# A graph network with sorted neighbour lists: heavy and light sorts as two stages, and a dense stage that starts ahead of its load

## The chip, the cores and the metric

The kernel runs on one core of a Trainium2 chip. A core has a matrix engine (PE; its weight loads are shown apart as PEld), a vector engine (DVE), an activation engine (ACT), a general engine (POOL) and a queue engine (SP) that here only issues DMAs. Each takes its instructions in the order in which the program has them and waits where one isn't ready. The metric is the device time of one call, in microseconds (us); lower is better.

## The reference, cut to what matters

A batch of 16 graphs, 1024 nodes, 64 channels, goes through four layers; each adds its result to x. All layers use the same adjacency matrix of a graph (1024 x 1024 float32, 4 MB a graph).

```python
h = relu(layernorm(x)); x = x + L0(h, adj)   # m = two dense layers of h; msg = relu(adj @ m); GRU cell of msg and h
h = relu(layernorm(x)); x = x + L1(h, adj)   # relu(D^-1/2 (adj + I) D^-1/2 (h @ kernel))
h = relu(layernorm(x)); x = x + L2(h, adj, nodemask)
h = relu(layernorm(x)); x = x + L3(h, adj)   # ((adj + I) @ h) / row sums
# L2: per node, a list of neighbours (its own node among them, some struck out by a dilation rule);
# per channel, the neighbours' values are sorted, and three quantiles are added up:
sv = sort(where(valid, x[:, None], big), axis=2)
agg = 0.25 * q(0.25) + 0.5 * q(0.5) + 0.25 * q(0.75)      # linear interpolation between two sorted values
out = (x + agg) @ W1 -> relu -> @ W2
```

The sort of L2 is what the change is about: every node has its own list, and all 64 channels of it are sorted apart.

## The kernel before, in words

Nodes are ranked by degree. The 128 nodes of highest degree ("heavy", in six classes, table HEAVY) have long lists; the seven other groups of 128 ("light") have at most 13 entries. A graph goes through stages, each written as a generator:

- fetch and load: the adjacency comes in as eight tiles of 128 x 1024 (tile a), PE transposes them, ACT copies them out (strip) and makes signs of them (sgn), and SP stores the transpose to DRAM (adjT).
- code, rank, cut, list: from the signs come degrees, ranks, the dilation and at last the lists of indices, idxH for heavy and idxL for light nodes, and weights that stand for the three quantiles.
- mid (`middle`, `dense01`, lines 1288 to 1382): layers 0 and 1. X is loaded, layernorm gives hm, two products give m2x; then adjT is read back in eight tiles (am) for the first adjacency product; the GRU cell (tiles rz, nn, d0) updates X; a second layernorm (tr), the second adjacency product, and X again; X is stored (x1), and a third layernorm's result h2 (another hm) is stored as the table tab.
- gath (`gathers`): POOL fetches rows of tab by index with indirect DMAs, one for 128 rows: 34 for the heavy lists into gh, which PE transposes and ACT copies into hb0; then 32 for the first light net into s0, 22 for the second into s1.
- sort (`sorts`): a heavy sort (tiles hb0 and hb1 in turn), then two light sorts (s0 with o0, s1 with o1). The steps are minima and maxima on DVE. hb1, o0 and o1 share one buffer, by the tag "other".
- sums: light keys are weighted (ACT) and added (DVE), and stored as agg; the heavy ones are summed within their sort.
- rear (`dense23`): layers 2 and 3; POOL gathers agg into rank order (zz, 8 indirect DMAs), then dense products, a layernorm (hr) and the third adjacency product, and the output.

No loop runs these. All stages of all 16 graphs go into one list at build time. `Order.run` (lines 223 to 248) takes again and again the stage whose next step can start first by the build's own estimate, and lets it issue that step; on a tie the earlier one in the list wins, which is sorted by the table `first` (0 for rear, sums and gath, 1 for mid and the lists, 2 for loads, 7 for the sorts). `yield after("name")` holds a stage back until the named stage or mark is done. So the order of instructions on each engine is fixed when the program is built, and any edit to stages, marks or buffers can move all of it. On the chip nothing is reordered.

Buffers: a tile's `bufs` says how many of it are there; the next one in turn waits for the readers of the one whose place it takes. LIGHTBUFS gives s0 and s1 two each, hb0 has two, X two, the t2 tiles of mid (nn, d0, tr, u1) two in common.

Every engine call goes through one helper, so the profile gives line 388 for nearly all instructions; they are told apart by their tiles.

Of the kernel before, what the change touches and what calls it, by code (L numbers as in the profile page):

```python
# [18 lines left out]
P = 128  # L19
EPS = 1e-5  # L20
STRIP = 1
DEPTH = 5
LIGHTBUFS = (2, 2)
SGN = 2
AM = 3
GH = 4
# [367 lines left out]
def kernel(  # L394
# [117 lines left out]
    def lists_for_all():  # L512
# [12 lines left out]
        def bank(dtype=F32):  # L525
            return ps1.take([P, 512 * 4 // mybir.dt.size(dtype)], dtype, "bank")
# [658 lines left out]

        def layernorm_relu(X, h=None, who="m", times=None):

            yield "V", X
            s = wp.tile([P, NT], F32, name="ln_s", bufs=2)
            V.reduce_sum(s, X, AX.X)  # L1190
            V.tensor_scalar(s, s, -1.0 / H, None, ALU.mult)
            yield "A", s
            v = wp.tile([P, NT], F32, name="ln_v", bufs=2)
            if h is None:
                h = wp.tile([P, NT, H], F32, name="h" + who, bufs=1)
            for t in range(NT):
                A.activation(h[:, t, :], X[:, t, :], AF.Square, bias=s[:, t : t + 1], accum_out=v[:, t : t + 1])
            A.activation(v, v, AF.Sqrt, bias=eps, scale=1.0 / H)
            yield "V", v
            V.reciprocal(v, v)  # L1200
            if times is not None:
                V.tensor_mul(v, v, times)
            V.tensor_mul(s, s, v)
            yield "A", s, v
            for t in range(NT):
                A.activation(h[:, t, :], X[:, t, :], AF.Relu, bias=s[:, t : t + 1], scale=v[:, t : t + 1])
            return h
# [4 lines left out]
                A.activation(dst[:, t, :], src[:, t, :], func, scale=by[:, t : t + 1])  # L1212

        def t2(name, who="m"):
            return wp.tile([P, NT, H], F32, name=name, tag="t2" + who, bufs=2 if who == "m" else 1)

        def transposed(h, dst):
            for i in range(NH):
# [67 lines left out]
            return pm  # L1286

        def dense01(b, S):
            X = wp.tile([P, NT, H], F32, name="X", bufs=2)
            S_.dma_start(X, x[b].rearrange("(t p) h -> p t h", p=P))  # L1290

            h = yield from layernorm_relu(X)
            cat = wp.tile([P, N], F32, name="cat")
            yield from transposed(h, cat[0:H, :])
            yield "T", cat
            m1T = wp.tile([P, N], F32, name="m1T", tag="big")
            pm = yield from product(w1, cat[0:H])
            yield from evicted(pm, m1T[0:H], AF.Relu, b1)
            yield "T", m1T
            p2 = yield from bank()  # L1300
            T.matmul(p2, *bias(0), start=True, stop=False)
            ams = streamed(b, 0)
            for t in range(NT):
                o = p2[:, t * H : (t + 1) * H]
                T.matmul(o, m1T[0:H, t * P : (t + 1) * P], w2, start=False, stop=t == NT - 1)
            yield "A", p2
            A.activation(m2x[:, :, 0:H], p2.rearrange("p (t h) -> p t h", h=H), AF.Relu)
            ps1.close(p2)
            pm = yield from propagated(b, m2x, 0, ams)

            yield "A", pm
            A.copy(m1T[H : H + 1, :], pm[H : H + 1, :])
            yield from evicted(pm, cat[H:P], AF.Relu)
            yield "T", m1T
            pr = yield from bank()
            for t in range(NT):
                T.transpose(
                    pr[:, t : t + 1], m1T[H : H + 1, t * P : (t + 1) * P], ident[H : H + 1, H : H + 1]
                )
            yield "V", pr  # L1320
            S["rs"] = rs = st.tile([P, NT], F32, name="rs")
            V.tensor_scalar(rs, pr[:, 0:NT], 1.0, None, ALU.add)
            ps1.close(pr)
            rz = wp.tile([P, NT, 2 * H], F32, name="rz", tag="big")
            nn = t2("nn")
            for g in range(2):
                yield "T", cat
                pg = yield from bank2()
                for i in range(4):
                    t = 4 * g + i  # L1330
                    o = pg[:, i * 4 * H : (i + 1) * 4 * H]
                    if i % 2 == 0:
                        T.matmul(pg[:, i * 4 * H : (i + 2) * 4 * H], *bias(2), start=True, stop=False)
                    T.matmul(o, cat[:, t * P : (t + 1) * P], wg, start=False, stop=i % 2 == 1)
                pgv = pg.rearrange("p (i c) -> p i c", c=4 * H)
                gs = slice(4 * g, 4 * g + 4)
                yield "A", pg
                A.activation(rz[:, gs, :], pgv[:, :, 0 : 2 * H], AF.Sigmoid)
                yield "V", rz
                V.tensor_mul(nn[:, gs, :], pgv[:, :, 2 * H : G], rz[:, gs, 0:H])  # L1340
                V.tensor_add(nn[:, gs, :], nn[:, gs, :], pgv[:, :, G : 4 * H])
                ps2.close(pg)
            yield "A", nn
            A.activation(nn, nn, AF.Tanh)
            yield "V", nn

            d0 = t2("d0")
            V.tensor_sub(d0, h, nn)
            V.tensor_mul(d0, d0, rz[:, :, H : 2 * H])
            V.tensor_add(d0, d0, nn)  # L1350
            V.tensor_add(X, X, d0)

            ams = streamed(b, 1)

            dinv = wp.tile([P, NT], F32, name="dinv", bufs=2)
            V.tensor_scalar(dinv, rs, 1e-30, None, ALU.max)
            yield "A", dinv
            A.activation(dinv, dinv, AF.Sqrt)
            yield "V", dinv
            V.reciprocal(dinv, dinv)  # L1360
            V.scalar_tensor_tensor(dinv, rs, 0.0, dinv, ALU.is_gt, ALU.mult)
            tr = yield from layernorm_relu(X, t2("tr"), "m", dinv)
            pm = yield from propagated(b, tr, 1, ams, own=True)
            g0 = wp.tile([P, N], F32, name="g0", tag="big")
            yield from evicted(pm, g0[0:H])
            yield "T", g0
            pm = yield from product(wk, g0[0:H])
            g1 = wp.tile([P, N], F32, name="g1", tag="big")
            yield from evicted(pm, g1[0:H])
            pa = yield from back(g1[0:H])  # L1370
            yield "A", pa
            u1 = t2("u1")
            scaled(u1, pa, dinv, AF.Relu)
            ps1.close(pa)
            yield "V", u1
            V.tensor_add(X, X, u1)

            yield "S", X
            S_.dma_start(D[b % DEPTH]["x1"].rearrange("(t p) h -> p t h", p=P), X)
            h2 = yield from layernorm_relu(X)  # L1380
            yield "S", h2
            S_.dma_start(D[b % DEPTH]["tab"][1 : N + 1, :].rearrange("(t p) h -> p t h", p=P), h2)
# [7 lines left out]
        def gather_heavy(b, S):  # L1390
# [1 line left out]
            d = D[b % DEPTH]  # L1392
            idxH = S["idxH"]
            yield "P", D[b % DEPTH]["tab"], idxH
            S["hb"] = hb = [qp.tile([P, NSLOT], F32, name="hb0", bufs=2), None]
            base = 0
            for _, nr, k, s, _, _ in HEAVY:
                if s > k:
# [210 lines left out]
        def sort_light(b, S, g):  # L1609
            ts, kept, _ = NETS[g]  # L1610
            n, width = USED[ts[0]], len(ts) * H
            plan = nets[g][0]
            bufs = [S["s", g], qp.tile([P, n * width], F32, name=f"o{g}", tag="other")]
            far(bufs[1], g, 1)

            def view(bf, first, stp, nr, ln, c):
# [147 lines left out]
        def middle(b, S):  # L1764
            if b:
                yield after(f"mid{b - 1}")
            yield after(f"load{b}")
            yield from dense01(b, S)

        def gathers(b, S):  # L1770
            yield after(f"list{b}", f"mid{b}")
            if b:
                yield after(f"gath{b - 1}")
            if b >= 2:
                yield after(f"heavy{b - 2}")
            yield from gather_heavy(b, S)
            yield f"gh{b}"
            for g in range(len(NETS)):
# [4 lines left out]

        def sorts(b, S):
            if b:
                yield after(f"sort{b - 1}")
            yield after(f"gh{b}")
            yield from sort_heavy(b, S)
            yield f"heavy{b}"
            for g in range(len(NETS)):  # L1790
                yield after(f"gl{b}.{g}")
                yield from sort_light(b, S, g)
                yield f"light{b}.{g}"
# [13 lines left out]
        for b in range(B):  # L1807
            S = {}
            for name, stage in (
                ("rear", rear), ("mid", middle), ("fetch", fetching), ("load", loads), ("code", coding), ("rank", ranking), ("cut", cutting), ("list", listing),  # L1810
                ("gath", gathers), ("sort", sorts), ("sums", sums),
            ):
                order.add(f"{name}{b}", stage(b, S))
        first = {"rear": 0, "sums": 0, "gath": 0, "conv": 1, "mid": 1, "list": 1, "cut": 1, "rank": 1, "code": 1, "load": 2, "fetch": 2, "sort": 7}
        order.stages.sort(key=lambda q: first[q[0].rstrip("0123456789")])
        with tc.manual_schedule():
            order.run()
# [383 lines left out]
```

## Time and profile before

| what | value |
| --- | --- |
| median of three runs | 2703.5 us (2701.03 to 2710.99) |
| profiled execution: time, span from first to last instruction | 2704.4 us, 2702.6 us |
| mean granted PE clock in it | 0.767 |
| heavy minima and maxima on DVE (hb from hb) | 728.2 us, 1072 instructions of one kind, 183.8 us of a second |
| light gathers, heavy gathers, zz gathers on POOL | 864, 544 and 128 |
| instructions in the trace | 34052 |

A profile line of a group reads: line, engine, operation, out<-in tiles, count, then busy time in us and mean ns of one, then the idle time of the engine just ahead of them and what ended most of it. "Issue" is time in which an engine waited for nothing that the profile shows. In a table of windows each row gives the stretch, its length, then busy time of each engine with the number of instructions, the granted PE clock, the share of DMA time, and GB/s. The row of slices has 40 digits, one for each fortieth of the span (67.6 us): 9 is 90% busy or more.

### The profile page before, as it was taken

To read this page: it belongs to the slowest core of one execution; us is meant where nothing else is said; L and a number is where in the kernel's file an instruction comes from. 1 tells how busy PE (TensorE), PEld (TensorE's weight loads), DVE (VectorE), ACT (ScalarE), POOL (GpSimd) and SP (SyncE) were. 2 spreads that over 40 slices of the span, in tenths; PEclk is the share of its full clock that TensorE was granted. 3 is DMA by queue.
4 is the path that set the end of the run, shared out by engine and by line. 5 is a ranking of instruction groups with operands and counts; after the bars stand their busy time and mean duration, and the time that the engine had idled before them with its cause. 6 is when DMAs were issued, how large, how long until landed. Compare 5 with 4: busy or idle time off the path is not lost.

```text
span 2702.6 us, 34052 instructions
## 1 busy us (share of the span) xinstructions
PE 1848.2 (68%) x8642; PEld 953.2 (35%) x8642; DVE 2269.5 (84%) x6486; ACT 1649.8 (61%) x5060; POOL 1777.8 (66%) x1598
## 2 busy tenths in 40 slices
PE   5866677757577776868677596768667778623354
PEld 3433343423334334334333343334233443311122
DVE  3438878998989969998986969999589898999991
ACT  7566685775767568485766767666575864522222
POOL 3037357676677878477777767777767767777721
PEclk7868677858788786978878696878778878765667
DMA  6556556655474664667566666557565744422312
GB/s 186 182 143 202 153 150 198 188 148 174 115 238 141 182 192 131 196 168 201 148 184 186 166 186 184 146 152 210 136 208 157 213 126 137 125 66 63 107 51 83
DMA packets 395184, 427.28 MB, mean 158 GB/s; under 512 B 165981, under 2 KB 302755, under 8 KB 394979
## 3 DMA queue, kind: packets, MB, share of 16 engines
q1 hardware_dynamic: 344386, 374.35, 44.4%
q0 software_dynamic: 50592, 50.66, 10.5%
q8 instruction: 72, 1.18, 0.2%
q14 instruction: 134, 1.09, 0.1%
HBM read 340.38 MB, written 84.46 MB: 157 GB/s over the span
## 4 chain that ended last, share of the span: by engine, by line
DVE 37%; PE 21%; POOL 14%; ACT 10%; DMA 9%; issue 8%; SPq 1%; POOLq 0%; DVEq 0%; ACTq 0%
PE bank L388 21%; DVE hb L388 16%; POOL s L388 9%; DVE s L388 5%; DMA am<-adjT 5%; DVE o L388 2%; POOL gh L388 2%; POOL zz L388 2%; ACT hm L388 2%; ACT junk L388 2%; ACT sgn L388 1%; DMA gh<-tab,idxH 1%; DVE ln_s L388 1%; DMA s<-tab,idxL 1%; DVE KH L388 1%
## 5 line engine op out<-in xcount | busy, mean ns | idle before, releaser
L388 POOL DMA_INDIRECT s<-tab,idxL x864 | 997.5, 1154 | 263.4 <-issue 255.5
L388 POOL DMA_INDIRECT gh<-tab,idxH x544 | 602.5, 1107 | 496.2 <-PE bank L388 173.4
L388 DVE TENSOR_TENSOR hb<-hb 128x128 f32<-128x128 f32 (+11 forms) x1072 | 728.2, 715 | 11.2 <-ACT hb L388 3.2
L388 PE MATMUL bank<-am,hr 128*64 128x512 f32 x512 | 269.0, 671 | 79.0 <-ACT hr L388 50.1
L388 PE MATMUL bank<-am,tr 128*64 128x512 f32 x512 | 266.0, 657 | 52.8 <-ACT tr L388 28.0
L388 PE MATMUL bank<-am,m2x 128*65 128x512 f32 x512 | 261.7, 651 | 33.4 <-DMA am<-adjT 29.7
L388 PE MATMUL bank<-ident,a 128*128 128x128 f32 x1024 | 201.7, 344 | 41.0 <-DMA a<-in_adj_dram 13.3
L388 POOL DMA_INDIRECT zz<-agg,posi x128 | 150.9, 1179 | 110.1 <-DMA agg<-s 62.3
L388 ACT ACTIVATE s<-s,wl 128x64 f32<-128x64 f32 x704 | 187.1, 344 | 47.6 <-DVE s L388 47.5
L388 ACT COPY strip<-bank 128x512 f32<-128x512 f32 x256 | 145.3, 587 | 70.0 <-PE bank L388 67.9
L388 DVE TENSOR_TENSOR hb<-hb,hb 128x656 f32<-128x656 f32 (+2 forms) x256 | 183.8, 731 | 3.9
L388 PEld LDWEIGHTS bank<-ident,a 128*128 128x128 f32 x1024 | 151.7, 178 | 81.1 <-issue 28.4
L388 PE MATMUL bank<-ident,gh 128*128 128x128 f32 x272 | 86.2, 343 | 114.5 <-DMA gh<-tab,idxH 92.1
L388 PE MATMUL bank<-ident,zz 128*64 128x128 f32 x256 | 66.5, 351 | 137.4 <-DMA zz<-agg,posi 122.7
L388 PEld LDWEIGHTS bank<-am,hr 128*64 128x64 f32 x512 | 71.7, 153 | 249.5 <-issue 147.2
L388 ACT ACTIVATE sgn<-strip 128x1024 bf16<-128x1024 f32 x128 | 135.2, 1056 | 30.4 <-issue 23.8
L388 ACT ACTIVATE junk<-bank,nkey 128x1024 bf16<-128x1024 f32 x128 | 141.3, 1120 | 6.7 <-PE bank L388 6.6
L388 PE MATMUL bank<-cx,oh 128*128 128x133 f16 (+1 forms) x1280 | 137.1, 254 | 6.4 <-DVE oh L388 6.4
L388 DVE TENSOR_TENSOR o<-s 128x1152 f32<-128x1152 f32 (+2 forms) x192 | 138.9, 752 | 2.2 <-DMA gh<-tab,idxH 0.4
L388 DVE TENSOR_TENSOR s<-s,o 128x576 f32<-128x576 f32 (+5 forms) x256 | 137.7, 548 | 3.3
L388 ACT ACTIVATE g<-bank 64x512 f32<-64x512 f32 x96 | 52.4, 585 | 141.6 <-PE bank L388 141.6
L388 ACT ACTIVATE sgn<-sgn 128x1024 bf16<-128x1024 bf16 x128 | 135.3, 1057 | 4.1
(345 smaller groups left out, 3984.4 us busy)
## 6 DMA issues: line engine op xcount, KB each, us to landing
am<-adjT SPq DMA_DIRECT2D x384, 512.0 KB
a<-in_adj_dram SPq DMA_DIRECT2D x128, 512.0 KB
adjT<-strip SPq DMA_DIRECT2D x128, 512.0 KB
s<-tab,idxL POOLq DMA_INDIRECT x864
gh<-tab,idxH POOLq DMA_INDIRECT x544
wb<-wd SPq DMA_DIRECT2D x32, 198.0 KB
X<-in_x_dram SPq DMA_DIRECT2D x16, 256.0 KB
x<-X SPq DMA_DIRECT2D x16, 256.0 KB
```

Of the source, the lines that this page charges most:

```text
L388: return f(*args, **kw)
```

## The change

The sort stage becomes two: `sorts` has the heavy sort alone, and follows the heavy sort of the graph before; `light_sorts` (stage "smalls") has the two light ones, and follows the light sorts of the graph before. The light nets' second buffer gets a tag of its own, so hb1 is no longer shared with o0 and o1. Room for it comes from one buffer fewer for s1, X and the t2 tiles, d0 computed in the place of h, and hr in the place of h2r. In `dense01` the wait for the graph's load moves from the start to the point ahead of the second dense product. HB names the number of hb0 buffers, which stays at 2.

```diff
-LIGHTBUFS = (2, 2)
+LIGHTBUFS = (2, 1)
+HB = 2
...
     def layernorm_relu(X, h=None, who="m", times=None):
-                h = wp.tile([P, NT, H], F32, name="h" + who, bufs=1)
+                h = wp.tile([P, NT, H], F32, name="h" + who, tag="h2r" if who == "r" else None, bufs=1)
...
     def t2(name, who="m"):
-            return wp.tile([P, NT, H], F32, name=name, tag="t2" + who, bufs=2 if who == "m" else 1)
+            return wp.tile([P, NT, H], F32, name=name, tag="t2" + who, bufs=1)
...
     def dense01(b, S):
-            X = wp.tile([P, NT, H], F32, name="X", bufs=2)
+            X = wp.tile([P, NT, H], F32, name="X", bufs=1)
...
             yield from evicted(pm, m1T[0:H], AF.Relu, b1)
             yield "T", m1T
+            yield after(f"load{b}")
             p2 = yield from bank()
...
-            d0 = t2("d0")
-            V.tensor_sub(d0, h, nn)
-            V.tensor_mul(d0, d0, rz[:, :, H : 2 * H])
-            V.tensor_add(d0, d0, nn)
-            V.tensor_add(X, X, d0)
+            V.tensor_sub(h, h, nn)
+            V.tensor_mul(h, h, rz[:, :, H : 2 * H])
+            V.tensor_add(h, h, nn)
+            V.tensor_add(X, X, h)
...
     def sort_light(b, S, g):
-            bufs = [S["s", g], qp.tile([P, n * width], F32, name=f"o{g}", tag="other")]
+            bufs = [S["s", g], qp.tile([P, n * width], F32, name=f"o{g}", tag="lighter", bufs=1)]
...
     def middle(b, S):
             if b:
                 yield after(f"mid{b - 1}")
-            yield after(f"load{b}")
             yield from dense01(b, S)
...
     def sorts(b, S):
             if b:
-                yield after(f"sort{b - 1}")
+                yield after(f"heavy{b - 1}")
             yield after(f"gh{b}")
             yield from sort_heavy(b, S)
             yield f"heavy{b}"
+
+    def light_sorts(b, S):
+            if b:
+                yield after(f"smalls{b - 1}")
             for g in range(len(NETS)):
                 yield after(f"gl{b}.{g}")
                 yield from sort_light(b, S, g)
...
-                ("gath", gathers), ("sort", sorts), ("sums", sums),
+                ("gath", gathers), ("sort", sorts), ("smalls", light_sorts), ("sums", sums),
...
-        first = {"rear": 0, "sums": 0, ..., "sort": 7}
+        first = {"rear": 0, "sums": 0, ..., "sort": 7, "smalls": 7}
```

More of the change, by code (lines that the diff above doesn't have):

```diff
@@ L1394, in gather_heavy @@
             yield "P", D[b % DEPTH]["tab"], idxH
-            S["hb"] = hb = [qp.tile([P, NSLOT], F32, name="hb0", bufs=2), None]
+            S["hb"] = hb = [qp.tile([P, NSLOT], F32, name="hb0", bufs=HB), None]
             base = 0
@@ L1773, in gathers @@
                 yield after(f"gath{b - 1}")
-            if b >= 2:
-                yield after(f"heavy{b - 2}")
+            if b >= HB:
+                yield after(f"heavy{b - HB}")
             yield from gather_heavy(b, S)
@@ L1810, in lists_for_all @@
                 ("rear", rear), ("mid", middle), ("fetch", fetching), ("load", loads), ("code", coding), ("rank", ranking), ("cut", cutting), ("list", listing),
-                ("gath", gathers), ("sort", sorts), ("sums", sums),
+                ("gath", gathers), ("sort", sorts), ("smalls", light_sorts), ("sums", sums),
             ):
                 order.add(f"{name}{b}", stage(b, S))
-        first = {"rear": 0, "sums": 0, "gath": 0, "conv": 1, "mid": 1, "list": 1, "cut": 1, "rank": 1, "code": 1, "load": 2, "fetch": 2, "sort": 7}
+        first = {"rear": 0, "sums": 0, "gath": 0, "conv": 1, "mid": 1, "list": 1, "cut": 1, "rank": 1, "code": 1, "load": 2, "fetch": 2, "sort": 7, "smalls": 7}
         order.stages.sort(key=lambda q: first[q[0].rstrip("0123456789")])
```

## The prediction, made before the changed kernel ran

> **What bounds the kernel now.** I read the page first: busy shares, the two rows of slices, the chain that ended last.
>
> ```profile
> PE 1848.2 (68%) x8642; PEld 953.2 (35%) x8642; DVE 2269.5 (84%) x6486; ACT 1649.8 (61%) x5060; POOL 1777.8 (66%) x1598
> DVE  3438878998989969998986969999589898999991
> POOL 3037357676677878477777767777767767777721
> DVE 37%; PE 21%; POOL 14%; ACT 10%; DMA 9%; issue 8%; SPq 1%; POOLq 0%; DVEq 0%; ACTq 0%
> L388 POOL DMA_INDIRECT s<-tab,idxL x864 | 997.5, 1154 | 263.4 <-issue 255.5
> L388 POOL DMA_INDIRECT gh<-tab,idxH x544 | 602.5, 1107 | 496.2 <-PE bank L388 173.4
> L388 POOL DMA_INDIRECT zz<-agg,posi x128 | 150.9, 1179 | 110.1 <-DMA agg<-s 62.3
> ```
>
> DVE has the most work, 2269.5 of 2702.6 us, yet the chain changes engine all the time: three pipelines run at nearly one pace. POOL is the second. A gather is 1.154 us plus 0.296 (255.5/864) of issue for light rows, 1.107 plus 0.23 for heavy ones, 1.18 plus 0.28 for zz. A graph has 54, 34 and 8 of them: 78.3 + 45.4 + 11.7 = 135.4 us, and 173.4/16 = 10.8 us of waiting for PE to free gh buffers makes 146. DVE's work is 2269.5/16 = 142 us a graph. Third is the dense chain `dense01`, one graph strictly after another.
>
> Then I cut the span where POOL starts the first heavy gather of graphs 0, 1, 2, ... 15, and at the last light gather (some rows shown; us, then busy time of each engine).
>
> ```profile
> core 0: us, PE busy (x) PEld busy (x) DVE busy (x) ACT busy (x) POOL busy (x), PEclk, DMA share, GB/s
> 157.00:332.00 175.00, 118.46 (x578) 61.18 (x578) 126.35 (x379) 111.61 (x299) 98.58 (x89) 0.76 0.59 175
> ...
> 1262.00:1409.00 147.00, 106.23 (x489) 53.00 (x490) 136.24 (x388) 101.02 (x311) 110.63 (x96) 0.78 0.61 176
> ...
> 1982.00:2130.00 148.00, 111.59 (x535) 56.31 (x534) 133.69 (x355) 98.78 (x307) 107.36 (x97) 0.84 0.62 183
> 2130.00:2282.00 152.00, 115.08 (x529) 56.14 (x526) 137.79 (x400) 94.67 (x303) 106.50 (x96) 0.80 0.56 159
> 2282.00:2435.00 153.00, 74.65 (x324) 36.86 (x324) 147.95 (x387) 62.94 (x236) 114.01 (x98) 0.72 0.35 90
> 2435.00:2590.00 155.00, 59.52 (x180) 30.52 (x180) 146.17 (x248) 39.51 (x155) 123.46 (x104) 0.58 0.29 77
> 2590.00:2703.00 113.00, 50.33 (x168) 22.99 (x168) 55.48 (x133) 32.65 (x127) 7.57 (x8) 0.70 0.24 76
> ```
>
> A graph costs about 150 us in the steady part. Up to 332 us DVE has idled 138 us (all columns up to there add to 194 busy), up to 1409 us 241, up to 2130 us 348: 14.7 us a graph in graphs 1 to 8, more later. The last light gather ends at 2590; heavy and light sorts of graph 15 still hold DVE until 2641, and 62 us of the last dense part follow.
>
> **The change, part by part.** What matters is the fixed order of each engine's instructions. I walked DVE's order in both built programs and gave every instruction the mean busy time of its kind in this profile (overlaps counted once, kinds with several shapes shared out by columns). DVE work that stands ahead of a point, without setup (14 us), comes out so. The end of the dense chain: graph 8 at 1108 before, 1151 after; graph 12 at 1615 and 1708; graph 13 at 1732 and 1871; graph 15 at 1969 and 2079. The first heavy sort instruction of graphs 8, 13 and 15: 1227, 1944, 2157 before, 1214, 1939, 2159 after. So the sorts keep their places, and the dense chains fall back among them. That is the price of the free sorts: once a heavy sort need not wait for the light one before it, it fills DVE time that carried the chains ahead.
>
> *Sorts in two stages.* Gain at the end: before, the heavy sort of graph 15 stands behind the light sort of 14, and light 15 behind heavy 15. After, light 15 is interleaved with heavy 15, and behind the last light gather only its second net's rest is left: 9.5 us of DVE and some scaling, 14 us, where the rows have 2641 - 2590 = 51. Bounds 10 and 51; I take 14, since DVE owes 90 us of sorting (59 heavy, 31 light) while POOL gathers light rows for 78.
>
> Smaller gain: DVE instructions that read what the one just ahead wrote fall from 1608 to 1428. The timeline prices that (start, duration):
>
> ```profile
> 98.94 0.69 DVE L388 TENSOR_TENSOR codes<-codes,bank 128x512 int32<-128x512 int32 x1 [0.67 <-ACT codes L388]
> 99.55 0.69 DVE L388 TENSOR_TENSOR d<-hm,nn 128x512 f32<-128x512 f32 x1
> 100.27 0.69 DVE L388 TENSOR_TENSOR d<-d,rz 128x512 f32<-128x512 f32 x1
> 101.00 0.69 DVE L388 TENSOR_TENSOR d<-d,nn 128x512 f32<-128x512 f32 x1
> ```
>
> An independent follower starts 0.61 us on, a dependent one 0.72: 0.11 each, 180 x 0.11 = 20 us in all, 16 of it by graph 13. Bounds 0 and 20. The Trainium skill, page "VectorE: DVE Perf Modes", section "The DRAIN you can't avoid", speaks against this term: the next operation starts only when the pipeline has emptied, whether or not instructions are chained. By that rule the term is nothing and the sum 16 us higher. The row differs, and I keep the row.
>
> *The cost.* In the profile POOL begins graph 13 when DVE has done 1782 us, 1768 without setup. After, gathers of graph 13 wait for its dense chain, with 1871 ahead: 103 more. At graphs 4 to 10 the two positions are within 40 of each other, and at graph 15 within 25, but by then POOL can't catch up, as it needs its own time for each graph.
>
> *The dense part ahead of the load.* From graph 1 on loads end well ahead (142 us against a start at 154; 979 against 1041), so it acts on graph 0 alone. ACT gets hm's squares, root, scaling and three pairs of evictions ahead of strips: 2.64 + 1.28 + 0.30 + 2.74 + 2.1 = 9 us, against about 10 us of ACT gaps there; and on SP the X load, 256 KB, now stands first, ahead of the mask and of all adjacency loads of 512 KB. I let the load end 3 us later. The first adjacency product then starts near 50 rather than 67 us. But gathers 0 also wait for the list's idxH, at 155; its chain gains only what rank's eight signs save by not sharing ACT with hm, 5 us. Bounds: 17 earlier and 9 later; I take 5 earlier.
>
> *One buffer for s1.* In POOL's queue the next graph's heavy gathers stand behind a blocked s1 gather. In DVE's order the light sort of the graph before ends within 20 us of where POOL reaches s1 in graphs 2, 3, 10 and 14. In the first three POOL waits for the dense chain anyway; in 14 DVE has 213 us of work ahead of that point and POOL needs 153 + 110 = 263. Nothing; without that cover 20 us each.
>
> *One X, one t2, h2r shared, d0 in place.* nn, tr and u1 live one after the other; hr is written after h2 was transposed; d0's four operations stay, 0.69 us each. The X load stands on SP behind the store of tab, which waits for the same hm; am loads and strip stores are behind it. Nothing; without this cover the 5.25 us that an X load shows in the chain, once a graph.
>
> *Sum, on the profiled span of 2702.6.* Start of gathers 13: 14 + 1871 - 16 + idle + 7 (hm's scaling, 2.7, and the store's landing) - 5. Idle: 348 if it is that of before at this point, 138 + 12 x 14.7 = 314 if the pace of graphs 1 to 8 holds, where sorts also followed their gathers at once. With 331 that is 2202, against 2130. Then three POOL rounds: 2590 - 2130 = 460 before, 3 x 146 = 439 with mean waits, 406 with none; I take 449. Then 14 and 62. 2202 + 449 + 14 + 62 = 2727. The profiled run took 2704.4, 1.8 over its span, and the median of the runs is 0.9 lower: 2728.
>
> **The rivals.** *Shorter drain alone* (faster): POOL keeps its starts. For it: DVE waited for ACT's hb copies only once, for 3.2 us, so gathers do run ahead of sorts. Against it: the 103 us at graph 13. Then 2435 + 63 + 12 + 78 + 14 + 62 = 2664. It decides by DVE's idle time up to graph 13: with 294 us the sum above gives 2690, with 268 it gives 2664.
>
> *Nothing that counts* (no change): a DVE at 84% with the same work and the same heavy sort positions ends where it did, as what is gained at the end is lost at graphs 12 and 13: about 2703. This is also the case in which decoupling does not do what it says, because heavy sorts start right behind their gathers (in graph 3 the gathers end at 701 us and the sort starts at 708) whether or not they wait for lights.
>
> **How the numbers follow.** Late dense chains 0.52, its own range 2695 to 2765 (idle 314 to 348, POOL rounds 430 to 460, the last sort up to 25); shorter drain 0.33; no change 0.15. A measurement tells 0.5% from none, so faster is below 2690 and slower above 2717. Of the first case 0.46 is slower and 0.06 in between; of the second 0.31 faster, 0.02 in between; of the third 0.09 in between and 0.03 on each side: 0.34, 0.17, 0.49. The range goes from 2645, under the rival's 2664, to 2780, where graph 13 idles as before, no dependent reads are saved and s1 blocks once.
>
> **What would show it.** In the new profile: graph 13's first heavy gather near 2200 us, POOL idle ahead of it for the dense chain (hm, tab); DVE done with the last sort 10 to 25 us after the last light gather; DVE idle 80 us or more after graph 13. The first adjacency product near 50 us, with gathers 0 hardly earlier. I'd be wrong if POOL starts graph 13 by 2150, or if DVE's idle time a graph is under 12 us.

## The result, and the profile after

| | before | after |
| --- | --- | --- |
| median of the runs on record, us | 2703.76 (20 runs) | 2703.33 (20 runs) |
| ratio, 95% interval | | 0.9989 (0.9974 to 1.0003) |
| profiled span, us; mean granted PE clock | 2702.6; 0.767 | 2705.8; 0.764 |
| first heavy gather of graphs 0, 1, 13, us | 157, 332, 2130 | 160, 323, 2187 |
| from gathers 13 to the end of the last light gather | 460 | 442 |
| from there to the end of the last sort | 51 | 15 |
| from there to the end of the span | 62 | 62 |

No change that a measurement could tell, where the forecast was 2728. The page of the changed kernel, first its busy line, two rows of slices and the chain:

```profile
PE 1840.9 (68%) x8642; PEld 960.9 (36%) x8642; DVE 2259.1 (83%) x6486; ACT 1647.5 (61%) x5058; POOL 1806.8 (67%) x1598
...
DVE  3458989999999979899798989898898987998381
...
POOL 4037367777877657577676777787676857778771
...
DVE 38%; PE 21%; DMA 12%; ACT 10%; POOL 10%; issue 7%; SPq 2%; DVEq 0%; POOLq 0%; ACTq 0%
...
L389 POOL DMA_INDIRECT s<-tab,idxL x864 | 1055.0, 1221 | 263.3 <-issue 256.9
L389 POOL DMA_INDIRECT gh<-tab,idxH x544 | 579.5, 1065 | 493.9 <-PE bank L389 166.5
```

DVE has 10 us less to do than before, POOL 29 more, with the same 1598 instructions: a light gather takes 1.221 us on average where it took 1.154, a heavy one 1.065 where it took 1.107. The slices show DVE dropping off in the last three (381, before 991): the last sorts no longer trail. The windows, cut where POOL starts gathers 0, 1, 7, 8, 12 to 15 and at the end of the last light gather (rows shown as in the prediction):

```profile
160.00:323.00 163.00, 113.29 (x594) 61.47 (x595) 122.88 (x384) 109.28 (x284) 96.33 (x88) 0.76 0.64 191
1258.00:1406.00 148.00, 113.19 (x569) 58.89 (x567) 128.30 (x358) 100.02 (x317) 105.22 (x97) 0.85 0.60 170
2022.00:2187.00 165.00, 122.24 (x583) 64.90 (x582) 151.34 (x441) 114.00 (x339) 111.55 (x96) 0.79 0.60 169
2187.00:2341.00 154.00, 115.30 (x503) 58.31 (x502) 133.18 (x388) 79.91 (x294) 107.80 (x96) 0.77 0.47 130
2341.00:2486.00 145.00, 81.42 (x231) 33.55 (x230) 133.18 (x319) 50.72 (x192) 115.10 (x96) 0.70 0.41 110
2486.00:2629.00 143.00, 38.78 (x148) 19.81 (x146) 91.88 (x171) 31.33 (x128) 113.87 (x96) 0.63 0.26 64
2629.00:2706.00 77.00, 30.22 (x112) 15.91 (x112) 20.84 (x54) 23.04 (x89) 7.55 (x8) 0.68 0.24 74
```

The balance is plain. Up to gathers 13 the changed kernel loses 57 us (2187 against 2130). From there it gains 18 in POOL's last three rounds and 36 in the last sort. DVE is full for 151 of 165 us in the round of graph 12, at whose end the dense chain of graph 13 is done 101 us later than before (2185 against 2084). In the last round DVE has 51 us to spare.

That chain releases gathers 13. SP issues the store of its result to tab, and POOL's first heavy gather of graph 13 follows (start, duration):

```profile
2184.37 0.36 SPq L389 DMA_DIRECT2D tab<-hm  x1
...
2187.43 0.95 POOL L389 DMA_INDIRECT gh<-tab,idxH  x1 [12.74 <-DVE o L389]
```

The profile puts the wait down to a DVE instruction, but the store's own semaphore comes at 2186.7, 0.8 us ahead of the gather, as it does for graphs 5, 7 and 8. So POOL stood ready at 2175 and waited 12.7 us for the chain (5.6 in the repeat below). The other 45 of the 57 us it was late by itself.

POOL's own account from gathers 1 to gathers 13 (my sum over its records) shows what made it late. The stretch is 1864 us against 1798: 66 longer, the 57 and the 9 by which gathers 1 start earlier. Light gathers are busy 788 against 750, heavy ones 439 against 447, zz 112 against 104 (96 of them against 88). Waits ahead of heavy gathers, without issue time, are 176 against 167, and ahead of zz 33 against 15; those for dense chains (graphs 5, 7, 8 and 13) are among the 176 with 36 us. No wait of over 1 us is ahead of light gathers in either kernel. The longer light gathers are the largest item.

What DVE waits for, in the changed kernel (in all, times, longest, us):

```profile
DVE hb L389 <- ACT hb L389: 25.8, 7, 10.4
DVE o L389 <- DMA s<-tab,idxL: 24.1, 6, 6.2
```

Heavy sorts now wait for the copies of their own gathers (before 3.2 us in all), light sorts for theirs: both run right behind POOL.

### The profile page after: what moved, and what is told of

Same layout as the page of the kernel before. It is cut to its first block, busy times and chain, and to the rows that moved or that the text cites. A ratio compares the mean times of both kernels' runs of the same rounds, so it can differ in the third digit from the quotient of the medians.

```text
span 2705.8 us, 34148 instructions
## 1 busy us (share of the span) xinstructions
PE 1840.9 (68%) x8642; PEld 960.9 (36%) x8642; DVE 2259.1 (83%) x6486; ACT 1647.5 (61%) x5058; POOL 1806.8 (67%) x1598
## 3 DMA queue, kind: packets, MB, share of 16 engines
q14 instruction: 133, 1.09, 0.1%
## 4 chain that ended last, share of the span: by engine, by line
DVE 38%; PE 21%; DMA 12%; ACT 10%; POOL 10%; issue 7%; SPq 2%; DVEq 0%; POOLq 0%; ACTq 0%
PE bank L389 21%; DVE hb L389 17%; DMA am<-adjT 6%; POOL s L389 5%; DVE s L389 4%; DVE o L389 3%; POOL gh L389 3%; SPq L389 2%; DMA gh<-tab,idxH 2%; ACT junk L389 1%; DVE ln_s L389 1%; ACT hm L389 1%; POOL zz L389 1%; ACT s L389 1%; ACT sgn L389 1%
## 5 line engine op out<-in xcount | busy, mean ns | idle before, releaser
L389 POOL DMA_INDIRECT s<-tab,idxL x864 | 1055.0, 1221 | 263.3 <-issue 256.9
L389 POOL DMA_INDIRECT gh<-tab,idxH x544 | 579.5, 1065 | 493.9 <-PE bank L389 166.5
L389 PE MATMUL bank<-am,tr 128*64 128x512 f32 x512 | 274.5, 679 | 79.6 <-DMA am<-adjT 40.4
L389 PE MATMUL bank<-ident,a 128*128 128x128 f32 x1024 | 195.3, 337 | 82.7 <-DMA a<-in_adj_dram 46.2
L389 POOL DMA_INDIRECT zz<-agg,posi x128 | 144.7, 1131 | 90.6 <-issue 34.1
L389 PEld LDWEIGHTS bank<-am,tr 128*64 128x64 f32 x512 | 71.9, 154 | 232.2 <-issue 131.8
L389 PE MATMUL bank<-cx,oh 128*128 128x133 f16 (+1 forms) x1280 | 144.7, 267 | 4.0 <-DVE oh L389 3.2
```

Source lines behind the costliest of these rows:

```text
L389: return f(*args, **kw)
```

## The experiments

Five sets. The kernel before ran beside each set on the same chip. In the first and the last it took 2710.2 and 2709.2 us. The three in between fell on other chips, where it took 3485 to 3511 us; what their traces show is told at the end. Their times are compared only within their sets, and they decide little about this change.

**First set: halves of the change.** The kernel before with the load's wait moved, and the changed kernel with it put back:

```diff
 # e1_load_only, from before; e2_split_only is the changed kernel with the reverse edit
+            yield after(f"load{b}")        # in dense01, ahead of the second product
-            yield after(f"load{b}")        # in middle, at the start
```

> Only the wait for the load is moved; sorts in one stage, buffers as before. Theory (drain won, dense chains lost, both from the split of the sorts): gathers of graph 0 start within 5 us of 157, gathers of graph 13 near 2130 (2105 to 2155), the last sort still ends some 50 us after the last light gather; 2690 to 2710. Rival (the moved wait wins what the split loses): 2685 or less. Rival (the moved wait alone loses): 2715 or more.

Measured: 2722.1, ratio 1.005 (1.0027 to 1.0072). Gathers 13 at 2204, not near 2130. Of the three outcomes it is the last.

> The wait for the load is back at the start of the dense part; sorts in two stages and buffers as in the changed kernel. Theory: its dense chain of graph 13 has 1846 us of DVE work ahead, so gathers of graph 13 start near 14 + 1846 + 310 + 7 = 2177 (2160 to 2195), the last sort ends 10 to 25 us after the last light gather, and the two cancel: 2690 to 2712. Rival (the split gains throughout, the moved wait costs it): 2685 or less.

Measured: 2735.8, ratio 1.0092 (1.0065 to 1.012), span 2735.9. Gathers 13 at 2210, the last light gather ends at 2658, the last sort at 2678. Both outcomes were missed.

Alone, each half makes the kernel slower, by 0.5 and 0.9%, and together they don't. What the moved wait does for the split kernel is seen early. This is POOL's wait between 214 and 350 us, first in the changed kernel, then in the one without the moved wait:

```profile
POOL gh L389 <- DVE idxH L389: 29.6, 1, 29.6
```

```profile
POOL gh L389 <- DVE idxH L389: 51.2, 1, 51.2
```

Both wait for the list of graph 1, but it comes 21 us later without the moved wait (344 against 323). ACT had done 107.3 us of work by the start of gathers 0 there (at 156 us), 115.8 in the changed kernel (at 160). So it is likely that the layernorm and evictions of graph 0, which fill the wait for the load, are out of the way when graph 1's list needs ACT. That isn't shown, as the two kernels differ in the order of every engine.

From there on the kernel without the moved wait is 12 to 50 us behind, and 23 at gathers 13 (2210 against 2187). What these wait for isn't the same, though. Without the moved wait the dense chain of graph 13 ends at 2194, its list at 2208, and POOL comes to gathers 13 from the gather before with 0.30 us in between: nothing holds them.

**Serial sorts, with the changed buffers.** In e4_serial the heavy sort waits for the light sorts of the graph before, and the light ones for the heavy sort of their own graph. In e4_last_free graph 15 is left out of that rule.

```diff
+FREE = 16                                  # e4_last_free: 15
-                yield after(f"heavy{b - 1}")
+                yield after(f"heavy{b - 1}" if b >= FREE else f"smalls{b - 1}")
...
+            if b < FREE:
+                yield after(f"heavy{b}")   # in light_sorts
```

> The changed kernel, but heavy sorts wait for the light sorts of the graph before and light ones for the heavy sort of their graph, as before. Its dense chain of graph 13 has 1684 us of DVE work ahead, its list 1792. Theory (the free sorts push the dense chains back): gathers of graph 13 start by POOL's own pace, 2110 to 2140, not near 2187; the last sort ends 40 to 55 us after the last light gather; 2680 to 2705. Rival (the smaller buffers push the chains back): gathers of graph 13 near 2187 and, with the long drain, 2735 or more.

Measured: 2781.6, ratio 1.0262 (1.0233 to 1.0292). The dense chains run ahead as expected: that of graph 13 ends at 2065, against 2185 in the changed kernel with the same buffers and the same moved wait. So it is the free sorts that push the chains back, and not the smaller buffers. Yet gathers 13 start at 2267. What POOL waits for ahead of light gathers in this kernel:

```profile
POOL s L390 <- ACT s L390: 47.9, 3, 23.8
POOL s L390 <- DVE hb L390: 47.7, 2, 38.5
POOL s L390 <- DMA agg<-s: 39.8, 2, 37.6
POOL s L390 <- DVE LF L390: 18.8, 1, 18.8
```

154 us in all ahead of light gathers, where the changed kernel has no wait of over 1 us. Each wait stands ahead of the 33rd light gather of a graph, the first into s1 (32 go into s0), and POOL's next heavy gathers queue behind it. That is the one s1 buffer, which is free only when the light sums of the graph before have been stored.

> As e4_serial, but the sorts of graph 15 are free of each other. The order is the same up to the last heavy sort. Theory: the dense chains stay where e4_serial has them, and the last sort ends 10 to 25 us after the last light gather instead of 40 to 55: 25 to 40 us below e4_serial, 2645 to 2675, faster than both kernels. Rival (times differ by the luck of the order alone, the drain is worth nothing): within 10 us of e4_serial.

Measured: 2786.2, ratio 1.0291 (1.0262 to 1.0321). Nothing gained, as the rival had it, though for another reason than luck: in the serial kernel the last heavy sort already starts right behind its gathers, so no sort trails whose order could be changed. The drain of before costs 51 us only because its last heavy sort starts 45 us after its gathers ended (2543 against 2498).

**Second and third set, on other chips.** One s1 buffer in the kernel before; the other smaller buffers without it; a reshuffle of the changed kernel by one number of the table of ties; the changed kernel with two s1 buffers.

```diff
-LIGHTBUFS = (2, 2)            # e7_s1_alone, from before
+LIGHTBUFS = (2, 1)
...
-"sort": 7, "smalls": 7}       # e6_tie, from the changed kernel
+"sort": 7, "smalls": 8}
...
-LIGHTBUFS = (2, 1)            # e9_s1_two, from the changed kernel
+LIGHTBUFS = (2, 2)
-strip = ap_.tile([P, NT, STRIP * P], F32, name="strip", bufs=2)
+strip = ap_.tile([P, NT, STRIP * P], F32, name="strip", bufs=1)
```

e8_others_small is before with the one X, the one t2, hr in h2r and d0 in place, as in the diff of the change.

> The kernel before with one buffer for s1 in place of two, nothing else. Theory A (the buffer is the hidden cost, and the split sorts pay it back): POOL waits 80 to 160 us in all ahead of light gathers, as in the serial kernel with the same buffers, and the time is 2740 to 2785. Theory B (each edit only reshuffles the order, and the time moves by the luck of that): hardly any wait of POOL ahead of light gathers, time 2690 to 2740, on either side of before.

> The kernel before with one X, one t2, hr in the place of h2r and d0 in the place of h, but two s1 buffers. The order of DVE's work is that of before to within 2 us. Both theories: no change, 2695 to 2715. If a wait for the single X or t2 costs something, up to 5 us a graph, it would be 2720 to 2780.

> The changed kernel with one number of the build's table of ties altered (light sorts 8 in place of 7): the same work, buffers and waits in another order of issue; the dense chain of graph 13 ends with 1787 us of DVE work ahead instead of 1871. Theory A: within 12 us of the changed kernel, 2692 to 2716. Theory B: off by as much as the two halves of the change were (12 to 32 us), on either side. The late-chain reasoning of the prediction: gathers 13 start 50 to 80 us earlier than 2187, near 2120, and the end 20 to 60 earlier.

> The changed kernel with two s1 buffers; room for it comes from one strip buffer fewer. Theory A: the split without its price, faster than before, 2640 to 2690. Theory B: anything from 2690 to 2740. A third view, that DVE's 2260 us of work and the idle time of the first graphs set the end whatever the sorts wait for: 2690 to 2715, unless the single strip slows the loads at the head by 10 to 20 us.

The set ran twice (e7b, e8b, e6b and e9b had the same expectations word for word), and the kernel before took 3495 and 3485 us in them:

| | second set, ratio | third set, ratio |
| --- | --- | --- |
| one s1 buffer | 0.9496 (0.94 to 0.9592) | 0.9603 (0.9533 to 0.9674) |
| other buffers smaller | 1.0075 (1.0011 to 1.0138) | 1.0105 (1.0037 to 1.0173) |
| tie | 0.9894 (0.9794 to 0.9995) | 0.9894 (0.9836 to 0.9952) |
| two s1 in the changed kernel | 0.9649 (0.9585 to 0.9712) | 0.964 (0.9586 to 0.9694) |

No time that was expected fits, because these chips stop for a reason of their own. The smaller X, t2 and h2r, which leave the order of DVE's work as it was, cost about 1% there. The tie, which was to show the luck of the order, has no run on a chip like that of the first set, so that rival stays open.

**Fourth set: gathers beside sorts** (before 3511 us). By then the longer light gathers stood as a third theory. e10 leaves the heavy minima and maxima of graphs 4 to 11 out, e11 gives those of the network one input tile.

```diff
 # e10_no_heavy, in sort_heavy
-            yield from network(net16, view)
+            if not 4 <= b < 12:            # the merges likewise
+                yield from network(net16, view)
 # e11_one_input, in network, for 4 <= b < 12
-                V.tensor_tensor(out, in0, in1, op)
+                V.tensor_scalar(out, in0, 1.0, None, op0=op)
```

> The changed kernel with two s1 buffers; room for it comes from one strip buffer fewer. Theory A (one s1 buffer is the price of the change): faster than before, 2640 to 2690. Theory B (only the order of issue counts): 2690 to 2740. Theory C (a gather on POOL is longer while DVE runs a heavy sort, and the free heavy sort stands right over the light gathers): no wait for s1 shows in the changed kernel, so the second buffer gives nothing, light gathers stay at 1.20 us or more, and the time is 2690 to 2720.

> The changed kernel with the minima and maxima of the heavy sorts left out in graphs 4 to 11, so that the output isn't the reference's. Theory C: light gathers of graphs 5 to 10 take 0.98 to 1.06 us instead of 1.22, those of graphs 1 to 3 and 13 to 15 as in the changed kernel, above 1.2. If their length comes from the transfers or from their own queue, it stays at 1.2 in all graphs.

> The changed kernel with every minimum and maximum of the first part of the heavy sort (the network, not the merges) in graphs 4 to 11 computed from one tile and a constant instead of two tiles: the same shapes and count, DVE as full, the output isn't the reference's. Theory C with two reads as its reason: light gathers beside these instructions take 0.95 to 1.05 us, the mean of graphs 5 to 10 falls from 1.22 to 1.08 to 1.15. If any busy DVE makes gathers longer, it stays at 1.18 or more.

Measured: e9c 3361, ratio 0.9619 (0.9545 to 0.9692); e10 3566 and e11 3497 in one run each. In e10 the light gathers of graphs 5 to 10 take 0.94 to 0.95 us and those of graphs 13 to 15 1.11 to 1.16. The direction is that of theory C; the sizes are lower than it said, and graphs 1 to 3 have 0.97 to 1.09 here in place of 1.2. In e11 the mean of graphs 5 to 10 is 0.98, but DVE stood idle too often on this chip for that mean to tell anything. The same can be read from any trace, without an experiment, by sorting all gathers (light, heavy and zz) by what DVE did during more than 80% of each, 90% for idle (mean us, number; my sums over the records):

| DVE meanwhile | before | after | e10 | e11 |
| --- | --- | --- | --- | --- |
| idle | 0.946 (118) | 0.943 (127) | 0.943 (769) | 0.943 (610) |
| heavy minima and maxima of two inputs | 1.289 (432) | 1.276 (411) | 1.260 (106) | 1.276 (147) |
| the same of one input | | | | 1.166 (22) |
| light sorts and sums of two inputs | 1.156 (188) | 1.135 (143) | 1.150 (76) | 1.151 (122) |
| other work | 1.016 (335) | 1.008 (324) | 1.011 (232) | 1.015 (214) |

Theory C holds as far as that gathers are longer beside sorts, though not with two reads as its only reason: the few gathers beside one-input instructions are longer too. The timeline of the changed kernel shows it (start, duration), POOL first, then DVE at the same places:

```profile
687.93 1.81 POOL L389 DMA_INDIRECT s<-tab,idxL  x1 [0.31 <-issue]
...
694.32 0.94 POOL L389 DMA_INDIRECT s<-tab,idxL  x1 [0.30 <-issue]
695.57 0.94 POOL L389 DMA_INDIRECT s<-tab,idxL  x1 [0.30 <-issue]
696.82 0.95 POOL L389 DMA_INDIRECT s<-tab,idxL  x1 [0.30 <-issue]
```

```profile
687.41 3.07 DVE L389 TENSOR_TENSOR hb<-hb 128x1312 f32<-128x1312 f32 x2
...
694.62 0.28 DVE L389 MAX8 LC<-mrc 16x8 f16<-16x128 f16 x1
...
696.03 0.27 DVE L389 MATCH_REPLACE8 mrc<-LC,mrc 16x128 f16<-16x128 f16 x1
```

Beside the large minima a gather takes 1.81, beside small work 0.94. The largest DVE share falls to heavy sorts in 489 of 864 light gathers after the change, in 347 before: the freed heavy sort starts at once, right over the light gathers of its graph.

**Fifth set, on a chip like that of the first** (before 2709.2 us): the changed kernel again, before with one s1 buffer, and the changed kernel with two.

> The changed kernel again, so that the two below stand beside it on one chip. Where before takes 2703 us: the same as before within 0.3%. On a chip where before takes 3490 us (late landings of gathers, all engines standing still meanwhile): below before by 2 to 4%, since the kernel with the same sorts and two s1 buffers was 3.5 to 4% below it there.

> Before with one s1 buffer. Theory A (one s1 buffer is the price of the change): where before takes 2703, 2740 to 2785. Theories B and C: 2690 to 2740. On a chip where before takes 3490: 4 to 5% below it, as in two sets before.

> The changed kernel with two s1 buffers and one strip buffer. Theory A: 15 to 60 us below the changed kernel of the same set. Theory C: within 15 us of it. On a chip where before takes 3490, theory A: 2% or more below the changed kernel; theory C: within 1% of it.

Measured: the changed kernel 2706.1, ratio 0.9974 (0.9947 to 1.0); one s1 buffer alone 2781.2, ratio 1.027 (1.0236 to 1.0304); two s1 buffers and one strip 2758.1, ratio 1.0171 (1.0125 to 1.0216).

The middle one is the clearest run of the study: one buffer fewer, 72 us. POOL's waits ahead of light gathers in it:

```profile
POOL s L388 <- ACT s L388: 90.8, 3, 52.0
POOL s L388 <- DVE hb L388: 20.9, 2, 20.6
POOL s L388 <- DMA agg<-s: 17.5, 2, 17.2
POOL s L388 <- DMA Xr<-x: 10.1, 1, 10.1
```

139 us of them, again all ahead of the first gather into s1; 102 come before gathers 13, which start at 2225, 95 us after those of before. The third kernel missed both theories, and its strip, shown ahead of that of the changed kernel, is the likely reason:

```profile
L389 ACT COPY strip<-bank 128x512 f32<-128x512 f32 x256 | 147.8, 592 | 242.6 <-DMA adjT<-strip 151.6 <-PE bank L389 90.5
```

```profile
L389 ACT COPY strip<-bank 128x512 f32<-128x512 f32 x256 | 144.6, 586 | 83.9 <-PE bank L389 71.0 <-DMA adjT<-strip 12.6
```

ACT waits 152 us for the store of the only strip, against 13. So this kernel doesn't tell what a second s1 buffer would be worth. Since the changed kernel has no wait for s1 in its trace, a second one has no wait to remove there; what it would do through another order wasn't measured. On chips of this kind no version that was tried is faster than both kernels.

Four of these runs have one s1 buffer and differ in the other two edits, the order of sorts and the place of the load's wait (medians, us; sets one and five, and the record for the changed kernel):

| | load's wait at the start | load's wait moved |
| --- | --- | --- |
| serial sorts | 2781 | 2782 |
| sorts in two stages | 2736 | 2703 |

With two s1 buffers and serial sorts they are 2709 (before) and 2722. So the buffer costs 72 us, the two stages give back 45 of it, and with them the moved wait is worth another 30 (2736 to 2706, on one chip). With serial sorts it is worth nothing, and with two s1 buffers as well it costs 12. The sum is nothing. The kernel in the first cell keeps the larger X, t2 and h2r, and hb1, o0 and o1 in one buffer. Each edit also comes with another order of all engines, and how much of a figure is the luck of that stays open without the tie.

## Why the prediction was wrong

**The step that failed** is a term of the sum, DVE's idle time up to gathers 13. "With 331" stood between 348, the idle time of before, and 314, the pace of graphs 1 to 8 carried on. Measured were 307 (304 in the repeat). It went wrong in graphs 8 to 12: up to gathers 8 DVE idles 241 us before and 237 after, so the sum left 90 for the rest. These rows, of before and then of the changed kernel, run from gathers 8 to gathers 13:

```profile
1409.00:2130.00 721.00, 535.64 (x2554) 276.99 (x2553) 613.61 (x1794) 473.33 (x1459) 531.13 (x473) 0.81 0.61 175
```

```profile
1406.00:2187.00 781.00, 569.25 (x2659) 295.78 (x2660) 710.73 (x2028) 522.99 (x1596) 556.46 (x480) 0.78 0.60 172
```

DVE idles 721 - 614 = 107 us in the first and 781 - 711 = 70 in the second, 14 a graph. So the early pace went on, the late graphs of before were no guide, and the middle between them was 20 us too high. With 307, in which the 5 us of the moved wait are contained, the sum is 14 + 1871 - 16 + 307 + 7 = 2183, where 2187 was measured. So the sum was 15 us off at gathers 13 (2202 against 2187), and another 7 lie in POOL's last three rounds, taken as 449 and measured as 442. The two make up nearly all of the 25 us that were forecast. Why DVE idles less there than before isn't shown. One thing that it depends on is the next term.

**The dense part ahead of the load**, "it acts on graph 0 alone", "I take 5 earlier". Against before the 5 is right in size: gathers 0 start 3 us later, gathers 1 start 9 earlier, and by then DVE has idled 133 us instead of 138. But the edit isn't confined to graph 0. With split sorts and without it, DVE idles 352 us up to gathers 13, and the kernel takes 30 us more. The sum had no term for what the edit does under the new order.

**Late dense chains**: right. DVE's work ahead of the end of graph 13's chain had been walked as 1732 and 1871 without 14 of setup; DVE had done 1746 and 1878 us by then. Gathers 13 wait for that chain. What the prediction didn't have is that POOL itself arrives 45 us late, so that the wait is 12.7 us and not most of the loss.

**Sorts in two stages**: 14 us after the last light gather were foreseen, 15 measured, and 62 of tail. POOL's last rounds took 442, where 449 was taken. *Dependent reads*: DVE's busy time fell by 10.4 us, half of the 20 that were priced; that it is due to them isn't shown. The price itself holds over the profile of before: of neighbouring 128x512 operations, 74 that read what the one ahead wrote start 0.03 us after its end, and 34 that don't 0.08 us before it (medians). The section of the Trainium skill that the prediction sets against this price, "The DRAIN you can't avoid" on the page "VectorE: DVE Perf Modes", goes on to say that an operation that isn't held starts earlier, so it doesn't rule the row out.

**One buffer for s1**, "Nothing; without that cover 20 us each": right for the changed kernel, whose trace has no such wait. But the cover is the split itself. Under serial sorts the same buffer costs 72 us, with waits of up to 52 us. The prediction saw in the split a gain of 37 at the end; the split also hides the buffer that was given up for it.

**Light gathers beside heavy sorts** were not in the sum. Light gathers take 57.5 us more of POOL's time (1055.0 against 997.5), and heavy gathers give 23 back. POOL's rounds from gathers 1 to 15 are 154.5 us each, against 150.2.

**One X, one t2, h2r shared, d0 in place**: priced at nothing, and not measured where it counts.

**The signs** that the prediction named nearly all came: gathers 13 near 2200 (2187), POOL idle ahead of them for tab, the last sort 15 us after the last light gather, DVE idle for 140 us after gathers 13, gathers 0 hardly moved. The first adjacency product moved from 67 to 56, not to 50. They were signs of the mechanism, and it came; none of them could tell 2728 from 2703.

**The rivals**: *nothing that counts* came true, and for the reason given, "what is gained at the end is lost at graphs 12 and 13": 54 gained, 57 lost, though the loss builds up from graph 9 on. It had 0.15. That the two come out so equal is luck as far as the runs show: without the moved wait, or with serial sorts and the changed buffers, they don't. *Shorter drain alone* needed idle time of 268 to 294 up to gathers 13; it was 307.

Open remains why the moved wait alone makes the kernel before slower by 0.5%. Its gathers 8 start 21 us ahead of those of before and its gathers 10 31 us behind. Between gathers 1 and 13 POOL waits 202 us ahead of heavy gathers, against 167, and 34 ahead of zz, against 15. A reshuffled order is likely, but it is not shown.

## What to carry to other kernels

A forecast of a small change can't rest on a large term whose bounds lie further apart than the change: here 25 us were forecast, and the middle was taken between 314 and 348. Price the room that a change takes as carefully as the change: take each buffer away alone, in the old order, since a buffer that "costs nothing" in the new order may be paid for by the whole of the gain. An edit at the head of the program isn't confined to the first graph. Where one engine's fixed order feeds another's queue, an edit's worth depends on the others: measure the corners of the table, not one edit after another.

## What the runs showed of the hardware

A gather that POOL issues takes 0.943 to 0.946 us on average while DVE stands idle (at most 0.96 over 127 in the changed kernel), and 1.26 to 1.29 beside heavy minima and maxima, at most 4.7. The Trainium skill, page "SBUF — State Buffer", section "SBUF: two separate sides", says that a vector instruction in a two-port mode, or one with two SBUF inputs where the GpSimd instruction reads SBUF, and a GpSimd instruction lock each other out of a shared pair of ports. The rows agree in direction. They show 0.32 to 0.34 us more on average, and some also beside one-input instructions, which may have been in such a mode; no run here shows that.

On three other chips the kernels took 3338 to 3566 us. Instructions of DVE and ACT were as long as in before (407 and 416 ns on average), those of PE hardly longer (374 against 365 ns; granted clock 0.70 against 0.77). The chain of waits of e8b_others_small, which runs DVE's work in the order of before:

```profile
PE 23%; DVE 20%; another core or an unknown queue 17%; ACT 15%; issue 13%; DMA 6%; POOL 5%; SPq 0%; DVEq 0%; POOLq 0%; ACTq 0%
```

PE, ACT and DVE stand still together for 327 us in stretches of over 4 us, nearly always while POOL issues light gathers; in before it is 9 us. In the same trace the next event on a light gather's semaphore after its start comes 2.2 us later in the middle case, much as in before (2.6), but 38.6 at the 99th percentile (5.7) and 69 at most (6). So gathers seem to land late there while more are issued; why wasn't found. One s1 buffer, which costs 2.7% on one kind of chip, is 4 to 5% faster on the other.
